# Five or six row tiles by address, shared by two queues, in a DIN recommender kernel

## The chip, the cores and the metric

The kernel runs on one core of a Trainium2 chip. The metric is the device time of one execution in microseconds (us). The median of three runs before the change is 31,618.79 us (31,618.49 to 31,619.22).

The engines are named as in the profile: PE (TensorE, with PEld for its weight loads), DVE (VectorE), ACT (ScalarE), POOL (GpSimd) and SP (SyncE). DMAs are issued by POOL, SP and ACT; ACTq and SPq are the instruction queues of ACT and SP, where an issued DMA appears.

## The reference

The inputs are 16,384 examples: an item, a category and a user id each, and a history of 200 item ids. Every id picks a row of 64 float32 values (256 bytes) from a table. For each of the 200 positions l, attention weights are computed for all 16,384 examples:

```
h   = i_emb[hist[l]]                      # 16384 x 64
x   = [h, it, h - it, h * it] @ au_W1 + au_b1      # it = i_emb[item], 36 columns
x   = dice(x)                             # normalised over the batch, sigmoid gate, alpha
w   = x @ au_W2 + au_b2
cur = cur + w * h
```

`dice(x)` normalises x over the whole batch, takes the sigmoid p of that, and gives p*x + (1-p)*alpha*x. After the history, a head of three layers (80, 40 and 2 columns), the first two with dice, works on user, item, category and `cur`. So the work is 200 times a gather of 16,384 rows, two small matrix products, and statistics over the batch.

## The kernel before

**Tiles.** The 16,384 examples are 128 tiles of 128. They are worked on in ND = 8 chunks of 16 tiles; a chunk is one (128 partitions x 1024) array after transposition. A step k is chunk c = k % 8 of position l = k // 8; the whole history is 1,600 steps. A loop (`For_i`, L455 and `steps`) runs four times over LPB = 45 positions, the last 20 positions and the head follow it.

**Where the rows come from.** `fetch(k)` gathers the 16 tiles of a chunk into `rows[k % 5]`, one indirect DMA on POOL per tile (L125). In four of the eight chunks (SIDES = 1, 3, 5, 7) the last tile is not gathered: `has_side`. Its 128 rows come one by one, 256 bytes each, by plain DMAs whose address is loaded from SBUF into a register (`addresses`, L268). The row numbers of these tiles are loaded per l (`load_addresses`), and multiplied by the row length on DVE (`scale_addresses`, L146) two steps later. Tiles of chunks 1 and 5 are SP's (`rows_by_sync`, L280, 32 rows per step, LOAD = 16 addresses per load, asked three steps ahead by `ask`), into `side`. Tiles of chunks 3 and 7 are ACT's (`rows_by_scalar`, L291, 32 rows per step in two halves, GROUP = 8 addresses per load), into `aside`. A semaphore per buffer of `aside` counts ACT's rows; `await_rows_by_scalar` waits for all 128. `turn(k)` then copies the tile into its place in `rows` on ACT (L339).

**A step.** The order on each engine is the order of the program (`manual_schedule`). Step k issues, in this order: fetch(k); gate(k-10) on ACT (sigmoid, L312) and weights(k-10), which is a product on DVE (L315) and the `wb` matmuls; half of ACT's rows; hidden(k-2) on ACT (L323, from `px` to `xs`) and measure(k-2), the batch statistics on DVE (L328); the other half of ACT's rows; turn(k-1): copy, four transposes on DVE (L154) and the `ph` and `px` matmuls; weigh(k-10) on DVE (L319, L320); product(k-1), a product on DVE (L345) and its `px` matmuls. After the last chunk of an l, moments() (L351 to L170) turns the statistics into scale and shift, with a root on ACT (L168), before gate reads them. LAG = 10 buffers `hT` and XR = 9 buffers `xs` carry a chunk from hidden to weigh.

**The head.** After the history, 256 gathers of category and user rows, then the three layers. In the second, `dice` for the first layer's second part (two arrays, `ab`) comes first; then per chunk a dice (L522 to L524), two matmuls with `w2a` over 128 rows (L538) and two with `w2b` over the 32 rows that belong to the chunk (L539), alternating; ACT moves the result out (L541) and DVE takes its statistics (L467).

Of the kernel before, what the change touches and what calls it, by code (L numbers as in the profile page):

```python
# [9 lines left out]
I32 = mybir.dt.int32  # L10
# [4 lines left out]
P = 128  # L15
D = 64
# [3 lines left out]
CD = 2 * CH  # L20
LPB = 45
ROWS = 5
LAG = 10
XR = 9
IDX = 3
BY_SP = (1, 5)
BY_ACT = (3, 7)
SIDES = (1, 3, 5, 7)
LOAD = 16
GROUP = 8  # L30
ROW = 4 * D
U8 = mybir.dt.uint8

# [2 lines left out]
def din_kernel(  # L36
# [32 lines left out]
    ZA = P // 2  # L69
    ZB = Z1 - ZA  # L70
    NS = len(SIDES)
    NB, NA = len(BY_SP), len(BY_ACT)
    serial = iter(range(10**6))
    NC = NT - NS
    BODY = L - L % LPB if L > LPB else 0
# [37 lines left out]
    idx = [make(f"idx{i}", P, NC, dt=I32) for i in range(IDX)]  # L113
    ids = [make(f"ids{i}", P, NT, dt=I32) for i in range(3)]
    side = [make(f"side{i}", P, D) for i in range(3)]
    aside = [make(f"aside{i}", P, D) for i in range(3)]
    landed = [tc.alloc_semaphore(f"landed{i}") for i in range(3)]
    addrs = make("addrs", 2 * S + 1, NS * P, dt=I32)
    addr = [addrs[i * S : i * S + 1] for i in range(3)]
    stats = [make(f"st{i}", P, 2 * ND, STATS) for i in range(3)]  # L120
    rstds = [make(f"rs{i}", P, 1) for i in range(3)]
# [15 lines left out]
    def load_hist_ids(i, l):  # L137
        nc.sync.dma_start(
            idx[i], r_hist[ds(l, 1), : NC * P].rearrange("l (p n) -> p (l n)", n=NC)
        )  # L140

    def load_addresses(i, l):
        nc.sync.dma_start(addr[i], r_hist[ds(l, 1), NC * P :])
# [74 lines left out]
    w1a = make("w1a", P, 4, P)  # L218
    w1b = make("w1b", P, 4, S)
    w2a = make("w2a", P, P)  # L220
    w2b = make("w2b", P, P)
    w3 = make("w3", P, 4, P)
    b1a = make("b1a", P, 1)
    b1b = make("b1b", S, 1)
# [9 lines left out]
    def head_weights():  # L234
        for t in (w1a, w1b, w2a, w2b, w3, bias2, al2):
            nc.vector.memset(t, 0.0)
        w1 = W1.rearrange("(f d) z -> d f z", d=D)
        for e in range(2):
            for g in range(2):
                r, d = quarter(e, g), ts(e, S)  # L240
                nc.sync.dma_start(w1a[r, :, ts(g, ZA)], w1[d, :, :ZA])
                nc.sync.dma_start(w1b[r, :, ts(g, ZB)], w1[d, :, ZA:])
        for g in range(2):
            nc.sync.dma_start(w2a[ts(g, ZA), g * ZA : g * ZA + Z2], W2[:ZA])
            nc.sync.dma_start(b1a[ts(g, ZA)], col(b1)[:ZA])
            nc.sync.dma_start(ala[ts(g, ZA)], col(alpha1)[:ZA])
            nc.sync.dma_start(b1b[ts(g, ZB)], col(b1)[ZA:])
            nc.sync.dma_start(bias2[g * ZA : g * ZA + Z2], col(b2))
            nc.sync.dma_start(al2[g * ZA : g * ZA + Z2], col(alpha2))
            for j in range(4):  # L250
                r = slice(j * S + g * ZB, j * S + (g + 1) * ZB)
                nc.sync.dma_start(w2b[r, g * ZA : g * ZA + Z2], W2[ZA:])
                w = j * S + g * ZO
                nc.sync.dma_start(w3[g * ZA : g * ZA + Z2, j, w : w + ZO], W3)
                nc.sync.dma_start(alb[r], col(alpha1)[ZA:])
        nc.sync.dma_start(bias3, b3.partition_broadcast(P))
        for t, u in ((ala, al1a), (alb, al1b), (al2, al12)):
            nc.vector.tensor_scalar(u, t, -1.0, 1.0, ALU.mult, ALU.add)

        for t, n in ((same_a, ZA), (same_b, ZB)):  # L260
            nc.vector.tensor_single_scalar(lane, lanes, n - 1, ALU.bitwise_and)
            nc.vector.tensor_copy(t, lane)
            nc.vector.tensor_scalar(t, t, 0.0, n / P, ALU.is_equal, ALU.mult)

    flat = i_emb.rearrange("v d -> (v d)").bitcast(U8)

    def addresses(l, s, p0, n, engine):
        _, at = nc.values_load_multi_w_load_instructions(  # L268
            addr[l % 3][:, s * P + p0 : s * P + p0 + n],
            engines=(engine,), min_val=0, max_val=ROW * (V - 1),  # L270
            skip_runtime_bounds_check_because="the DMA checks the address against the table",
        )
        return [flat[ds(a, ROW)].rearrange("(o d) -> o d", o=1) for a in at]

    def rows_by_sync(m, part, n):
        l, j = divmod(m, NB)
        s, dst = SIDES.index(BY_SP[j]), side[m % 3].bitcast(U8)
        for p0 in range(part * n, part * n + n, LOAD):
            for j, row in enumerate(addresses(l, s, p0, LOAD, mybir.EngineType.SP)):
                nc.sync.dma_start(dst[p0 + j : p0 + j + 1], row)  # L280


    keys = {}

    def rows_by_scalar(m, part):
        l, j = divmod(m, NA)
        s, dst = SIDES.index(BY_ACT[j]), aside[m % 3].bitcast(U8)
        key = keys.setdefault(m, f"rows{next(serial)}")
        for j, row in enumerate(addresses(l, s, part * GROUP, GROUP, mybir.EngineType.Activation)):
            p = part * GROUP + j  # L290
            dma = nc.scalar.dma_start(dst[p : p + 1], row).then_inc(landed[m % 3], 16)  # L291
            tc.no_tile_sem_insts.add(dma.ins.name)
            tc.add_to_no_dep_group(key, dma.ins)

    def await_rows_by_scalar(m):
        if m in keys:
            fence = nc.scalar.wait_ge(landed[m % 3], 16 * P)
            tc.declare_fence(fence.ins, group=keys.pop(m))
            nc.scalar.sem_clear(landed[m % 3])

    def has_side(k):
        return k % ND in SIDES

    def fetch(k):
        l, c = divmod(k, ND)
        for n in range(TD - has_side(k)):
            j = column(c, n)
            gather(rows[k % ROWS], idx[l % IDX][:, j : j + 1], n, i_emb)

    def gate(k):  # L310
        i = k // ND % 3
# [15 lines left out]
        for i in range(2):  # L327
            nc.vector.bn_stats(stats[l % 3][:, 2 * c + i, :], xs[k % XR][:, ts(i, CH)])  # L328

    def turn(k):  # L330
        if has_side(k):
            l, c = divmod(k, ND)
            if c in BY_ACT:
                m = l * NA + BY_ACT.index(c)
                await_rows_by_scalar(m)
                of = aside[m % 3]
            else:
                of = side[(l * NB + BY_SP.index(c)) % 3]
            nc.scalar.copy(rows[k % ROWS][:, TD - 1], of)  # L339
        transpose(hT[k % LAG], rows[k % ROWS])  # L340
        layer(ph, [(unit, hT[k % LAG])])
        layer(px, [(blk_h, hT[k % LAG]), (blk_i, itT[k % ND])], last=False)
# [25 lines left out]
    def step(k, last=None):  # L368

        def has(j):  # L370
            return last is None or j <= last

        if has(k):
            fetch(k)
        if has(k - LAG):
            gate(k - LAG)
            weights(k - LAG)
        if has(k):
            scalar_rows(k, 0)
        if has(k - 2):  # L380
            hidden(k - 2)
            measure(k - 2)
        if has(k):
            scalar_rows(k, 1)
        if has(k - 1):
            turn(k - 1)
        if has(k - LAG):
            weigh(k - LAG)
        if has(k - 1):
            product(k - 1)  # L390
        if has(k - 2) and (k - 2) % ND == ND - 1:
            moments((k - 2) // ND)

    AHEAD = ND // NB - 1 - BY_SP[0]

    def ask(k, end):
        m, part = divmod(k + 1 + AHEAD, ND // NB)
        if m < end * NB:  # L400
            rows_by_sync(m, part, P * NB // ND)

    def scalar_rows(k, slot):
        m, part = divmod(k, ND // NA)
        n = P * NA // ND // GROUP
        for i in range(n)[slot::2]:
            rows_by_scalar(m, part * n + i)

    def steps(l0, n, end):
        for k in range(n * ND):  # L410
            l, c = divmod(k, ND)
            if c == 0 and l + 1 < end:
                load_hist_ids((l + 1) % IDX, l0 + l + 1)
            if c == 2 and l + 1 < end:
                load_addresses((l + 1) % 3, l0 + l + 1)
            if c == 4 and l + 1 < end:
                scale_addresses((l + 1) % 3)
            ask(k, end)
            step(k)

    with tc.manual_schedule():
# [4 lines left out]
        load_ids(ids[2], r_user)  # L426
        nc.gpsimd.iota(lanes, pattern=[[1, P]], base=P, channel_multiplier=-1)
        attention_weights()
        for t in (*hT, *xs, *side, *aside, hm):
            nc.vector.memset(t, 0.0)  # L430
        for t in curT:
            nc.vector.memset(t, 0.0)
# [14 lines left out]
            if c:  # L447
                transpose(itT[c - 1], rows[(c - 1) % ROWS])
        nc.vector.memset(rows[-1 % ROWS], 0.0)
        for k in range(-1 - AHEAD, 0):  # L450
            ask(k, L)
        head_weights()

    if BODY:
        with tc.For_i(0, BODY, LPB) as l0:  # L455
            with tc.manual_schedule():
                steps(l0, LPB, LPB + 1)
                await_rows_by_scalar(LPB * NA - 1)

    K = (L - BODY) * ND  # L460
    za = [hT[(K - LAG + c) % LAG] for c in range(ND)]
# [28 lines left out]
    with tc.manual_schedule():  # L490
# [36 lines left out]
        z2 = itT  # L527
        na, nb = head_moments(0, same_a), head_moments(1, same_b)
        ab = ucT[:2]
        for j in range(2):  # L530
            dice(ab[j], zb[j], nb, al1b, alb)
        for c in range(ND + 1):
            if c < ND:
                dice(curT[c], za[c], na, al1a, ala)
                q = ts(c % 4, S)
                for h in range(2):
                    cols = ts(h, CH)
                    nc.tensor.matmul(pz[c % 4][:, cols], w2a, curT[c][:, cols], start=True, stop=False)  # L538
                    nc.tensor.matmul(pz[c % 4][:, cols], w2b[q], ab[c // 4][q, cols], start=False, stop=True)  # L539
            if c:  # L540
                nc.scalar.activation(z2[c - 1], pz[(c - 1) % 4], AF.Identity, bias=bias2)  # L541
                measure_head(2, c - 1, z2[c - 1])

        n2 = head_moments(2, same_a)
        for c in range(ND):
# [56 lines left out]
```

## Time and profile before

| | |
|---|---|
| median of the runs | 31,618.79 us |
| the profiled execution's own time | 31,616.96 us |
| its span, first to last instruction | 31,615.1 us |
| mean granted clock of PE | 0.81 |
| gathers on POOL, history | 24,800 of 944 ns |
| gathers on POOL, items and head | 384 (3 x 128) |
| row DMAs on ACT, on SP | 51,200 and 51,200 |
| DMA share of 16 engines, gathers | 11.8% |

The busy time of an engine leaves out register loads and the issue of DMAs: for ACT and SP, whose queues issue 102,400 row DMAs, it has to be read from the queue rows of the timeline. For POOL the time from the start of one gather to the start of the next matters, not the busy time alone. The page cuts the span into 40 slices; they are alike from second to last, so a stretch from the middle stands for the history.

### The profile page before, as it was taken

To read this page: it belongs to the slowest core of one execution; us is meant where nothing else is said; L and a number is where in the kernel's file an instruction comes from. 1 tells how busy PE (TensorE), PEld (TensorE's weight loads), DVE (VectorE), ACT (ScalarE), POOL (GpSimd) and SP (SyncE) were. 2 spreads that over 40 slices of the span, in tenths; PEclk is the share of its full clock that TensorE was granted. 3 is DMA by queue.
4 is the path that set the end of the run, shared out by engine and by line. 5 is a ranking of instruction groups with operands and counts; after the bars stand their busy time and mean duration, and the time that the engine had idled before them with its cause. 6 is when DMAs were issued, how large, how long until landed. Compare 5 with 4: busy or idle time off the path is not lost. (4 is left out here: it accounts for less than half of the span.)

```text
span 31615.1 us, 357535 instructions
## 1 busy us (share of the span) xinstructions
PE 20448.2 (65%) x38864; PEld 8357.2 (26%) x38864; DVE 15015.4 (47%) x18963; ACT 4479.6 (14%) x4670; POOL 23766.1 (75%) x25189
## 2 busy tenths in 40 slices
PE   5666666666666666666666666666666666666666
PEld 2222222222222222222222222222222222222222
DVE  4444444444444444444444444444444444444443
ACT  1111111111111111111111111111111111111111
POOL 7777777777777777777777777777777777777776
PEclk7888888888888888888888888888888888888887
DMA  1111111111111111111111111111111111111111
GB/s 29 28 28 28 28 28 28 28 28 28 28 28 28 28 28 28 28 28 28 28 28 28 28 28 28 28 28 28 28 28 28 28 28 28 28 28 28 28 28 23
DMA packets 1050292, 890.26 MB, mean 28 GB/s; under 512 B 644640, under 2 KB 644640, under 8 KB 1047784
## 3 DMA queue, kind: packets, MB, share of 16 engines
q0 software_dynamic: 805888, 826.84, 11.8%
q1 hardware_dynamic: 138920, 27.05, 0.4%
q10 hardware_dynamic: 102976, 13.32, 0.3%
q14 instruction: 2202, 18.04, 0.2%
q8 instruction: 306, 5.01, 0.1%
HBM read 865.03 MB, written 0.13 MB: 27 GB/s over the span
## 5 line engine op out<-in xcount | busy, mean ns | idle before, releaser
L125 POOL DMA_INDIRECT rows<-in_L_rec_i_emb,idx x24800 | 23403.2, 944 | 7593.5 <-issue 7032.1
L159 PE MATMUL ph<-hT,unit 128*128 128x512 f32 x6404 | 5658.4, 1029 | 10498.9 <-DVE hT L154 10498.9
L154 DVE STREAM_TRANSPOSE hT<-rows 64x512 f32<-64x512 f32 x6404 | 4518.8, 706 | 8256.8 <-DMA rows<-in_L_rec_i_emb,idx 4150.3
L328 DVE BATCH_NORM_STATS2 st<-xs 128x6 f32<-128x512 f32 x3204 | 2060.4, 685 | 7172.9 <-ACT xs L323 7172.9
L159 PEld LDWEIGHTS ph<-hT,unit 128*128 128x128 f32 x6404 | 1688.5, 295 | 13506.4 <-DVE hT L154 13334.4
L159 PE MATMUL px<-hT,blk_h 128*128 128x512 f32 x6404 | 3936.6, 702 | 0.0
L323 ACT ACTIVATE xs<-px,au_bias 128x1024 f32<-128x1024 f32 x1602 | 1784.3, 1114 | 14626.1 <-PE px L159 12323.9
L159 PE MATMUL wb<-y,blk_p 128*128 128x512 f32 x6440 | 3329.8, 599 | 455.3 <-DVE y L315 455.3
L159 PE MATMUL px<-itT,blk_i 128*128 128x512 f32 x6404 | 3368.8, 608 | 0.0
L159 PE MATMUL wb<-xs,blk_x 128*128 128x512 f32 x6440 | 3307.3, 595 | 51.5 <-PEq L455 39.9
L159 PE MATMUL px<-hm,blk_m 128*128 128x512 f32 x6408 | 3013.0, 592 | 40.5 <-DVE hm L430 40.5
L312 ACT ACTIVATE pg<-xs,sh,rs 128x1024 f32<-128x1024 f32 x1610 | 1939.8, 1205 | 3751.2 <-issue 2579.9
L315 DVE TENSOR_TENSOR y<-pg,xs 128x1024 f32<-128x1024 f32 x1610 | 1956.6, 1215 | 512.9 <-ACT pg L312 508.6
L159 PEld LDWEIGHTS px<-hT,blk_h 128*128 128x128 f32 x6404 | 1566.7, 245 | 2295.1 <-issue 2294.6
L319 DVE SCALAR_TENSOR_TENSOR wb<-wb,au_bias,hT 128x1024 f32<-128x1024 f32 x1610 | 2080.5, 1292 | 88.2 <-PE wb L159 36.0
L320 DVE TENSOR_TENSOR curT<-wb,curT 128x1024 f32<-128x1024 f32 x1610 | 1970.8, 1224 | 54.8
L345 DVE TENSOR_TENSOR hm<-ph,itT 128x1024 f32<-128x1024 f32 x1601 | 1941.2, 1212 | 0.0
L159 PEld LDWEIGHTS px<-itT,blk_i 128*128 128x128 f32 x6404 | 1374.9, 215 | 1925.3 <-issue 1925.3
L159 PEld LDWEIGHTS wb<-y,blk_p 128*128 128x128 f32 x6440 | 1212.0, 191 | 2081.7 <-issue 1445.9
L159 PEld LDWEIGHTS wb<-xs,blk_x 128*128 128x128 f32 x6440 | 1228.3, 191 | 1603.9 <-issue 1597.9
L159 PEld LDWEIGHTS px<-hm,blk_m 128*128 128x128 f32 x6408 | 1218.1, 190 | 1573.0 <-issue 1424.7
L339 ACT COPY rows<-aside 128x64 f32<-128x64 f32 x401 | 97.9, 244 | 2659.6 <-DMA aside<-in_L_rec_i_emb 2525.7
(155 smaller groups left out, 2171.5 us busy)
## 6 DMA issues: line engine op xcount, KB each, us to landing
aside<-in_L_rec_i_emb ACTq DMA_DIRECT2D x51200, 0.2 KB
side<-in_L_rec_i_emb SPq DMA_DIRECT2D x51200, 0.2 KB
rows<-in_L_rec_i_emb,idx POOLq DMA_INDIRECT x24800, 2.4
idx<-in_r_hist SPq DMA_DIRECT2D x200, 62.0 KB
addrs<-in_r_hist SPq DMA_DIRECT2D x200, 2.0 KB
rows<-in_L_rec_i_emb,ids POOLq DMA_INDIRECT x128, 2.4
rows<-in_L_rec_c_emb,ids POOLq DMA_INDIRECT x128, 2.4
rows<-in_L_rec_u_emb,ids POOLq DMA_INDIRECT x128, 2.4
```

Source lines behind the costliest of these rows:

```text
L125: nc.gpsimd.indirect_dma_start(out=dst[:, n, :], out_offset=None, in_=table, in_offset=bass.IndirectOffsetOnAxis(ap=ids, axis=0),)
L154: nc.vector.transpose(by_tile(dst[ts(e, D)], i), of[ts(i, D), :, ts(e, S)])
L159: nc.tensor.matmul(dst[:, ts(i, CH)], lhsT, rhs[:, ts(i, CH)], start=(first and j == 0), stop=(last and j == len(pairs) - 1), skip_group_c ...
L312: nc.scalar.activation(pg, xs[k % XR], AF.Sigmoid, bias=shifts[i], scale=rstds[i])
L315: nc.vector.tensor_mul(y, pg, xs[k % XR])
L319: nc.vector.scalar_tensor_tensor(wb, wb, au_bias2, hT[k % LAG], ALU.add, ALU.mult)
L320: nc.vector.tensor_add(curT[k % ND], wb, curT[k % ND])
L323: nc.scalar.activation(xs[k % XR], px, AF.Identity, bias=au_bias)
L328: nc.vector.bn_stats(stats[l % 3][:, 2 * c + i, :], xs[k % XR][:, ts(i, CH)])
L339: nc.scalar.copy(rows[k % ROWS][:, TD - 1], of)
L345: nc.vector.tensor_mul(hm, ph, itT[k % ND])
```

## The change

The change moves more tiles from POOL to the two row queues, puts both queues on the same tile, and rearranges the step and the second layer of the head.

- SIDES becomes (1, 3, 4, 5, 6, 7), with SOMETIMES = 5 and EACH = 3: chunk 5's last tile comes by address only where l % 3 == 0. So six tiles come by address in every third l, five in the others. In these, chunk 5's last tile is gathered with ids of its own (`sidx`, loaded by `load_side_ids`).
- `rows_by_address(k)` takes the place of `rows_by_sync`, `rows_by_scalar`, `ask` and `scalar_rows`. Each step asks for a step's share (an eighth) of the l's own rows, half on SP and half on ACT: 40 each with five tiles, 48 with six. Addresses are loaded 20 at a time (16 with six tiles). Both write to the three buffers `side`; the semaphore counts the rows of both.
- `place(k)`, the wait and the copy, is taken out of turn and stands in front of the step's rows on ACT. hidden(k-2) goes to the front of the step, gate follows it, weights goes to the end beside weigh, after product. measure(k-2) follows turn(k-1), but in the step that ends an l it comes first, with moments().
- LAG becomes 9 and XR 8, `aside` is dropped.
- In the second layer `w2b` is laid out as four 128-row matrices that are zero outside a chunk's 32 rows, so all matmuls have 128 rows. The dice of `ab` comes when it is first needed, and the move out of PSUM is two chunks behind.

```diff
-LAG = 10
-XR = 9
+LAG = 9
+XR = 8
 IDX = 3
-BY_SP = (1, 5)
-BY_ACT = (3, 7)
-SIDES = (1, 3, 5, 7)
-LOAD = 16
-GROUP = 8
+SIDES = (1, 3, 4, 5, 6, 7)
+SOMETIMES = 5
+EACH = 3
+LOAD = 20
...
+    def load_side_ids(i, l):
+        j = column(SOMETIMES, TD - 1)
+        nc.sync.dma_start(sidx[i], r_hist[ds(l, 1), j * P : (j + 1) * P].rearrange("l p -> p l"))
...
+    def rows_by_address(k):
+        l, s = divmod(k, ND)
+        first, tiles = tiles_by_address(l)
+        n = len(tiles) * P // ND // 2
+        loads = -(-n // LOAD)
+        for i, (engine, issue) in enumerate(
+            ((mybir.EngineType.SP, nc.sync), (mybir.EngineType.Activation, nc.scalar))
+        ):
+            r0, end = (2 * s + i) * n, (2 * s + i + 1) * n
+            while r0 < end:
+                many = min(end - r0, -(-n // loads))
+                at0 = tiles[r0 // P] * P + r0 % P
+                while tiles[(r0 + many - 1) // P] * P + (r0 + many - 1) % P != at0 + many - 1:
+                    many -= 1
+                _, at = nc.values_load_multi_w_load_instructions(
+                    addr[l % 3][:, at0 : at0 + many],
...
+                for r, a in enumerate(at, r0):
+                    m, p = first + r // P, r % P
+                    key = keys.setdefault(m, f"rows{next(serial)}")
+                    dma = issue.dma_start(
+                        side[m % 3].bitcast(U8)[p : p + 1],
+                        flat[ds(a, ROW)].rearrange("(o d) -> o d", o=1),
+                    ).then_inc(landed[m % 3], 16)
...
     def has_side(k):
-        return k % ND in SIDES
+        l, c = divmod(k, ND)
+        return c in SIDES and (c != SOMETIMES or l % EACH == 0)
...
+        ends = (k - 2) % ND == ND - 1
         if has(k):
             fetch(k)
+        if has(k - 2):
+            hidden(k - 2)
+            if ends:
+                measure(k - 2)
+                moments((k - 2) // ND)
         if has(k - LAG):
             gate(k - LAG)
-            weights(k - LAG)
+        if has(k - 1):
+            place(k - 1)
         if has(k):
-            scalar_rows(k, 0)
-        if has(k - 2):
-            hidden(k - 2)
-            measure(k - 2)
-        if has(k):
-            scalar_rows(k, 1)
+            rows_by_address(k)
         if has(k - 1):
             turn(k - 1)
-        if has(k - LAG):
-            weigh(k - LAG)
+        if has(k - 2) and not ends:
+            measure(k - 2)
         if has(k - 1):
             product(k - 1)
-        if has(k - 2) and (k - 2) % ND == ND - 1:
-            moments((k - 2) // ND)
...
+        if has(k - LAG):
+            weights(k - LAG)
+            weigh(k - LAG)
...
-        for j in range(2):
-            dice(ab[j], zb[j], nb, al1b, alb)
-        for c in range(ND + 1):
+        for c in range(ND + 2):
             if c < ND:
                 dice(curT[c], za[c], na, al1a, ala)
-                q = ts(c % 4, S)
-                for h in range(2):
-                    cols = ts(h, CH)
-                    nc.tensor.matmul(pz[c % 4][:, cols], w2a, curT[c][:, cols], start=True, stop=False)
-                    nc.tensor.matmul(pz[c % 4][:, cols], w2b[q], ab[c // 4][q, cols], start=False, stop=True)
-            if c:
-                nc.scalar.activation(z2[c - 1], pz[(c - 1) % 4], AF.Identity, bias=bias2)
-                measure_head(2, c - 1, z2[c - 1])
+                layer(pz[c % 4], [(w2a, curT[c])], last=False)
+                if c % 4 == 0:
+                    dice(ab[c // 4], zb[c // 4], nb, al1b, alb)
+                layer(pz[c % 4], [(w2b[:, c % 4], ab[c // 4])], first=False)
+            if c >= 2:
+                nc.scalar.activation(z2[c - 2], pz[(c - 2) % 4], AF.Identity, bias=bias2)
+                measure_head(2, c - 2, z2[c - 2])
```

## The prediction

> **What bounds the kernel now.** I read the page's busy shares and costliest groups first, then the waits, then the timeline in three places: ACT's own rows in mid-kernel, SP's, and the end of the kernel.
>
> ```profile
> PE 20448.2 (65%) x38864; PEld 8357.2 (26%) x38864; DVE 15015.4 (47%) x18963; ACT 4479.6 (14%) x4670; POOL 23766.1 (75%) x25189
> ...
> L125 POOL DMA_INDIRECT rows<-in_L_rec_i_emb,idx x24800 | 23403.2, 944 | 7593.5 <-issue 7032.1
> ...
> POOL rows L125 <- issue: 7142.1, 23320, 9.3
> ...
> POOL rows L125 <- DMA rows<-in_L_rec_i_emb,idx: 548.0, 1797, 0.3
> ...
> 7129.46 0.94 POOL L125 DMA_INDIRECT rows<-in_L_rec_i_emb,idx  x1 [0.30 <-issue]
> 7139.70 0.94 POOL L125 DMA_INDIRECT rows<-in_L_rec_i_emb,idx  x1 [9.30 <-issue]
> 7140.95 0.94 POOL L125 DMA_INDIRECT rows<-in_L_rec_i_emb,idx  x1 [0.30 <-issue]
> ```
>
> POOL looks 75% busy but is full. A gather takes 944 ns and the gap before the next is 0.30 us, "issue", so gathers start every 1.249 us (7139.70 to 7140.95 is one such step). The waits put down to DMAs are also 0.3 us each at most: that gap under another name. The only larger gaps are four turns of the loop: from single records 10.25, 8.46, 8.45 and 3.9 us between starts, 26 us beyond the usual. The account closes: 24,800 gathers plus 384 for items and head are 25,184 x 1.249 = 31,455; plus 2.9 before the first, 26 at the turns and 136 after the last start (31477.85) makes 31,620 against a span of 31,615.1. So time is the number of gathers, and what follows the last.
>
> ```profile
> 15018.10 1.11 ACT L323 ACTIVATE xs<-px,au_bias 128x1024 f32<-128x1024 f32 x1 [9.41 <-PE px L159]
> 15018.96 6.68 ACTq L291 DMA_DIRECT2D aside<-in_L_rec_i_emb  x16
> ...
> 15045.20 0.24 ACT L339 COPY rows<-aside 128x64 f32<-128x64 f32 x1 [6.20 <-DMA aside<-in_L_rec_i_emb]
> 15045.35 1.20 ACT L312 ACTIVATE pg<-xs,sh,rs 128x1024 f32<-128x1024 f32 x1
> 15046.09 6.65 ACTq L291 DMA_DIRECT2D aside<-in_L_rec_i_emb  x16
> ...
> SPq L268 <- DVE addrs L146: 6115.7, 132, 48.4
> SPq L268 <- DVE y L315: 3216.8, 66, 49.7
> 15153.09 25.15 SPq L280 DMA_DIRECT2D side<-in_L_rec_i_emb  x64
> ```
>
> The page's 14% for ACT leaves out its queue (ACTq). Sixteen row DMAs take 6.2 to 6.7 us there, and 0.86 us pass between an activation's start and the first row: the load of eight addresses into registers. The queue goes on while an activation runs (15045.35 lasts 1.20, the rows start 0.74 into it), so an activation costs the queue almost nothing. SP waits 9,332 us for addresses, 30% of the span, and needs 25.15 us for 64 rows with the loads between them.
>
> ```profile
> 31504.35 2.05 PE L538 MATMUL px<-curT,w2a 128*128 128x512 f32 x2 [9.48 <-issue]
> 31506.33 2.07 PE L539 MATMUL px<-ucT,w2b 32*128 32x512 f32 x2
> 31508.33 2.08 PE L538 MATMUL px<-curT,w2a 128*128 128x512 f32 x2
> 31510.33 2.07 PE L539 MATMUL px<-ucT,w2b 32*128 32x512 f32 x2
> ```
>
> In the second layer every switch between a 128-row and a 32-row matmul costs: one starts each 2.0 us.
>
> **The change, part by part.**
>
> *Gathers.* Before, 124 per l. After, 122 where six tiles come by address and 123 where five do. Four bodies of 45 l and a tail of 20 have 4 x 15 + 7 = 67 l of the first kind and 133 of the second: 8,174 + 16,359 = 24,533, which is 267 fewer. 267 x 1.249 = **-333.5 us**, on the path, as POOL is never starved.
>
> *Row DMAs on ACT.* 256 rows per l for both queues become 768 or 640 shared evenly: 48 or 40 per step on each. Prices from ACT's single records: row to row 0.3165 us (median 0.307); from a load's first row to the second 0.555, so 0.24 extra; load to first row 0.945 for 8 addresses, and 1.364 on SP for 16. That is 0.052 per address, so I estimate 1.36 for ACT's loads of 16 and 1.57 for 20. With six tiles: 384 x 0.3165 + 24 x (0.24 + 1.36) = 160; events and dispatch of two activations and a copy about 3; the wait at the moments about 6 (activation 1.11, two statistics 1.3, aggregate to variance 2.25, root 0.3, then reciprocal and shift; bounds 5.4, and 8 if the 2.5 of L319 and L320 stand before it). Together 169, against POOL's 122 x 1.249 = 152.4. With five: 320 x 0.3165 + 17 x 1.81 + 3 + 6 = 141 (the 17th load is at the skipped column), against 153.6. Three l: **ACT 451, POOL 459.6**, a margin of 9 us or 2%.
>
> ACT falls 16 us behind in each first l and wins 25 back in the next two. What takes the lag up is the ring of five rows buffers: a gather of step k waits for the transposes of k-5, which now end some 5 us after the gathers of that step, so 4 x 19.1 - 5 = 71 us stand free. I take ACT at nothing. Its bounds: with row to row at 0.307, ACT needs 441; at 0.337 (the mean while SP issues too, every long interval counted) 472.
>
> *SP.* 48 rows with three loads: 3 x (1.364 + 0.367 + 14 x 0.33 + 0.28) = 19.9 us; 40 with two 16.3. Three l with index, address and the new sidx loads (0.43 each, as for a 128x1 load of ids at the start): about 435, 95% of POOL. Behind SP stand only rows; behind a late row stand ACT's wait in place(), then DVE's transposes. Price nothing by the same ring.
>
> *Order and buffers.* LAG 10 to 9, XR 9 to 8, and weights behind product. On DVE one step is still 2.9 + 1.4 + 1.2 + 1.2 + 1.3 + 1.2 = 9.2 us. L339's activation of k-2 writes the buffer that the wb matmuls of k-10 read at the end of step k-1, so it starts after them: in the trace the last wb matmul ended 13.8 us after the transposes began (15007.62 to 15021.44). With the 2.5 of weigh that chain is 16.3 per step, under 19.1. Price nothing; covered by POOL, at 16.3 of 19.1. The SP look-ahead (ask) goes: each tile is now asked within its own l, one step or more before place(). At loop exit SP first issues the head's weights (21 us, 28061 to 28082): the ring again. The scale of 768 addresses, not 512, adds about 0.2 us of DVE per l, hidden.
>
> *Second layer.* 32 matmuls at 2.0 are 64 us (31504.35 to 31568.5). All with 128 rows and no switch they start 0.86 us apart, as the wb ones do in mid-kernel: 27.5. Then DVE is last: ten dice of 2.03 (L523 0.81, L524 1.22) and eight pairs of statistics of 1.29 are 30.6 from 31498.2; with the last matmuls, activation (1.1) and statistics behind curT[7], the end of L467 moves from 31570.97 to about 31531: **-40 us**. Bounds: 0 if the switch was not the cause, -42 if DVE alone counts.
>
> *Turns of the loop.* 26 us stay, since after two five-tile l ACT has caught up; if it has not, up to one step each, 4 x 19 = 77.
>
> Sum: 31,615.1 - 333.5 - 40 = 31,242 of span. The profiled run's own time is 1.8 above its span and the runs' median 1.8 above that (31,618.79): **31,246 us**, 1.2% faster. Its own range is 31,215 to 31,330.
>
> [...] The row first: ACT's median from row to row is 0.308 us with SP issuing within 0.4 us and 0.307 alone; SP's is 0.323 both ways. [...] Were the 0.217 us of each row exclusive, a pair would take 0.434, ACT 120 us more per three l, and the kernel some 38,000 us; the row speaks against that, and I go by it.
>
> **Rivals.**
>
> *ACT becomes the bound.* For it: 2% is a thin margin, the loads of 20 addresses are an extrapolation, and both queues now issue nearly all the time, not SP 70% of it. Against: the 0.307 above. Place: ACTq in rows_by_address, whence late place() and late transposes. At 0.337 per row ACT needs 472 per three l: 12.4 over POOL, 67 times = 830 us, and about 60 at the turns: **32,130 us**, slower. It decides from 459.6 on; from 465 on (0.330 per row) the loss eats the whole gain.
>
> *The step's chain becomes the bound.* hidden(k-2) behind wb(k-10), product behind ph: if the chain of 16.3 were 19.4, 1,600 steps x 0.3 = 480 us more: **31,730 us**. Against: its matmul spacings are measured, and 2.8 us are free.
>
> *It does not do what it says:* POOL's gathers grow with more DMAs in flight and eat the 333. At 1.262 (the 99th percentile now) 24,917 gathers cost 324 more: **31,570 us**. Against: 1.249 holds in stretches with and without rows.
>
> **How the numbers follow.** Forecast 72%; ACT as bound 19%, a sixth of it still under 31,550; the chain 5%; larger gathers 4%. The range 31,215 to 31,680 takes in the forecast, the mild part of ACT as bound and the larger gathers: some 81%. What this kernel's measurement tells from no change is 0.2%, 63 us. Faster: 72 + 3, 75%; same: half of the gathers' rival and a little of ACT's, 4%; slower: 21%.
>
> **What would show it.** Right: 24,533 gathers still 1.249 us apart, no POOL gap over 1 us but the turns, ACTq idle some 2%, about 40 us less after the last gather, wb matmuls of the second layer near 0.86 apart. Wrong: POOL's rows waiting for DVE hT (the ring is empty), with ACTq solid from six-tile l to six-tile l; or turns of 30 us and more.

## The result, and the profile after

The changed kernel takes 31,252.28 us in the median of four runs (31,247.28 to 31,267.21), the kernel before 31,618.9: a ratio of 0.9885, with a 95% interval of 0.9868 to 0.9902. It is 1.2% faster; 31,246 was forecast. The profiled execution is the slowest of the four, 31,267.21 us with a span of 31,265.4. One execution of the kernel with the old second layer, below, took 44,256 us at a granted clock of 0.528 in place of 0.80 and is left out of its median.

The first lines are the busy shares and the group of the gathers, from the page of the changed kernel; then its waits on POOL (us in total, times, longest us).

```profile
PE 20664.2 (66%) x38856; PEld 8483.2 (27%) x38856; DVE 15126.3 (48%) x18955; ACT 4402.8 (14%) x4941; POOL 23531.5 (75%) x24922
...
L123 POOL DMA_INDIRECT rows<-in_L_rec_i_emb,idx x24400 | 23043.1, 944 | 7477.2 <-issue 7226.7
```

```profile
POOL rows L123 <- issue: 7379.5, 24090, 17.2
POOL rows L123 <- DMA rows<-in_L_rec_i_emb,idx: 171.5, 562, 0.3
POOL rows L123 <- DVE hT L156: 16.8, 55, 0.3
```

POOL is as full as before. The 24,400 gathers here and 133 by `sidx` make 24,533, and the gap between two is still 0.3 us. No wait for DVE hT is longer than that: the ring of rows buffers was never empty. The larger gaps are the four turns of the loop: 17.2 us at the first, 4.4, 4.5 and 3.2 at the others. Here is the first in POOL's timeline (start, duration, and in brackets the idle time before):

```profile
7060.08 0.94 POOL L123 DMA_INDIRECT rows<-in_L_rec_i_emb,idx  x1 [0.30 <-issue]
7078.19 0.94 POOL L123 DMA_INDIRECT rows<-in_L_rec_i_emb,idx  x1 [17.16 <-issue]
7079.43 0.94 POOL L123 DMA_INDIRECT rows<-in_L_rec_i_emb,idx  x1 [0.30 <-issue]
```

The second layer in PE's timeline, where x4 in a row are two of the matmuls that had a row with x2 each before:

```profile
31195.82 1.88 PE L161 MATMUL ph<-curT,w2a 128*128 128x512 f32 x4
31197.54 1.88 PE L161 MATMUL ph<-ucT,w2b 128*128 128x512 f32 x4
31199.26 1.88 PE L161 MATMUL pg<-curT,w2a 128*128 128x512 f32 x4
```

These rows start 1.72 us apart, so one matmul takes 0.86; before, one took 2.0.

The difference of the two spans can be split up from single records. Of 349.7 us (31,615.1 to 31,265.4), 267 gathers x 1.249 are 333.5, and the time after the last gather's start fell from 137.3 (for which the prediction has 136) to 97.8, 39.5. Against that the turns cost 28.1 in place of 26.1, gathers longer than 1 us cost 20.0 in place of 2.7, and the 3.9 that remain are the spread of all other starts: 333.5 + 39.5 - 2.0 - 17.3 - 3.9 = 349.8.

ACT in mid-kernel, in its timeline (ACTq rows are runs of row DMAs; the time in brackets counts as idle also what the queue spends on issuing):

```profile
15089.70 1.11 ACT L339 ACTIVATE xs<-px,au_bias 128x1024 f32<-128x1024 f32 x1 [16.18 <-DVE wb L335]
15090.83 1.28 ACT L170 ACT_TABLE_LOAD   x1
15094.63 0.29 ACT L170 ACTIVATE std<-var,eps 128x1 f32<-128x1 f32 x1 [2.52 <-DVE var L380]
15094.94 1.28 ACT L328 ACT_TABLE_LOAD   x1
15096.24 1.21 ACT L328 ACTIVATE pg<-xs,sh,rs 128x1024 f32<-128x1024 f32 x1
15096.90 14.98 ACTq L301 DMA_DIRECT2D side<-in_L_rec_i_emb  x40
15111.98 1.11 ACT L339 ACTIVATE xs<-px,au_bias 128x1024 f32<-128x1024 f32 x1 [14.53 <-issue]
```

This is a step that ends an l. From 15089.70 to 15096.90 the queue issues no rows, because of the moments; then it issues 40 rows and their loads, and the next step's hidden starts 0.1 us behind them. In all steps, the time in which ACT had issued its rows and waited for px is 201 us, 0.6% of the span. POOL sets the time, and ACT is close behind it.

### The profile page after: what moved, and what is told of

Same layout as the page of the kernel before. It is cut to its first block, busy times and chain, and to the rows that moved or that the text cites. A ratio compares the mean times of both kernels' runs of the same rounds, so it can differ in the third digit from the quotient of the medians.

```text
span 31265.4 us, 423966 instructions
## 1 busy us (share of the span) xinstructions
PE 20664.2 (66%) x38856; PEld 8483.2 (27%) x38856; DVE 15126.3 (48%) x18955; ACT 4402.8 (14%) x4941; POOL 23531.5 (75%) x24922
## 3 DMA queue, kind: packets, MB, share of 16 engines
q0 software_dynamic: 797344, 818.07, 14.9%
## 5 line engine op out<-in xcount | busy, mean ns | idle before, releaser
L123 POOL DMA_INDIRECT rows<-in_L_rec_i_emb,idx x24400 | 23043.1, 944 | 7477.2 <-issue 7226.7
L161 PE MATMUL ph<-hT,unit 128*128 128x512 f32 x6404 | 5876.4, 1065 | 10398.4 <-DVE hT L156 10395.6
L161 PE MATMUL px<-hT,blk_h 128*128 128x512 f32 x6404 | 4090.6, 727 | 0.0
L161 PEld LDWEIGHTS px<-hT,blk_h 128*128 128x128 f32 x6404 | 1641.9, 256 | 2404.6 <-issue 2394.2
L352 ACT COPY rows<-side 128x64 f32<-128x64 f32 x1068 | 249.0, 233 | 327.0 <-DMA side<-in_L_rec_i_emb 197.0
```

Source lines behind the costliest of these rows:

```text
L123: nc.gpsimd.indirect_dma_start(out=dst[:, n, :], out_offset=None, in_=table, in_offset=bass.IndirectOffsetOnAxis(ap=ids, axis=0),)
L161: nc.tensor.matmul(dst[:, ts(i, CH)], lhsT, rhs[:, ts(i, CH)], start=(first and j == 0), stop=(last and j == len(pairs) - 1), skip_group_c ...
```

## Experiments

All times are medians, beside runs of the kernel before on the same chip (31,618 to 31,621 us). The kernels ran on several chips, so a difference of some 3 us between two of them tells nothing.

**Five tiles in every l.** This changes the number of gathers and takes the load off ACT.

```diff
+SIX = ()
...
-        return c in SIDES and (c != SOMETIMES or l % EACH == 0)
+        return c in SIDES and (c != SOMETIMES or l % EACH in SIX)
```

> Five tiles by address in every l, never six: 123 gathers per l, 24,984 with items and head, 67 more than the changed kernel; ACT has 141 us of work per l against POOL's 153.6. If POOL's gathers alone set the time: 67 x 1.249 = 84 us slower than the changed kernel, 31,336 us. If the six-tile l already cost ACT more than the ring of rows buffers hides, taking them out gives something back: less than 31,300 us, and the trace of the changed kernel's gaps on POOL shrinks by more than its turns.

Measured 31,334.87 us, 82.6 more than the changed kernel (ratio to before 0.991, 0.9894 to 0.9925). The law of the gathers holds to 1 us; ACT now waited 2,302 us for px and this bought nothing.

**Six tiles in two of three l.**

```diff
+SIX = (0, 1)
-LOAD = 20
+LOAD = 24
...
-        return c in SIDES and (c != SOMETIMES or l % EACH == 0)
+        return c in SIDES and (c != SOMETIMES or l % EACH in SIX)
```

> Six tiles in two of every three l (67 gathers fewer than the changed kernel), addresses loaded 24 at a time, which makes ACT's six-tile l cheaper (two loads per step for three). If POOL alone set the time it would be 31,252 - 84 = 31,168 us. By the prediction's ACT account three l now cost ACT 2 x 163 + 141 = 467 us against POOL's 458.4: 8.6 us too much, 67 times, 31,740 us (31,500 to 31,950), with POOL's rows waiting for DVE hT.

Measured 32,625.83 us (ratio 1.0316, 1.0302 to 1.0331): slower than before, although it has 67 gathers fewer than the changed kernel. The rival "ACT becomes the bound" lies one notch away. Its waits:

```profile
POOL rows L124 <- issue: 7370.1, 23510, 64.2
...
POOL rows L124 <- DVE hT L157: 1390.3, 521, 6.9
...
ACT rows L353 <- DMA side<-in_L_rec_i_emb: 284.1, 148, 7.5
```

POOL waits for the transposes (DVE hT), up to 6.9 us each, and at every turn 64 us: ACT's lag fills the whole ring. But the size was off by 886 us. A mean step takes 20.05 us here without the turns, 481 per three l, of which ACT waits for px only about 1; the account said 467. Its timeline at the start of an l shows a part that was left out:

```profile
15112.75 1.20 ACT L329 ACTIVATE pg<-xs,sh,rs 128x1024 f32<-128x1024 f32 x1
15118.36 0.24 ACT L353 COPY rows<-side 128x64 f32<-128x64 f32 x1 [4.41 <-DMA side<-in_L_rec_i_emb]
15120.18 18.42 ACTq L302 DMA_DIRECT2D side<-in_L_rec_i_emb  x48
```

The copy of place() stands 4.41 us for the rows of the l's last tile, which both queues finished asking for only at the end of the step before. All of the next 48 rows are queued behind it.

**The same, with the rows asked a step ahead.**

```diff
-        if has(k):
-            rows_by_address(k)
+        for j in asked:
+            rows_by_address(j)
...
-            step(k)
+            step(k, asked=[j for j in ((0, 1) if k == 0 else (k + 1,)) if j < n * ND])
```

> The kernel with six tiles in two of three l, with each step asking for the rows of the next step's share (the first step of a stretch asks for two). In that kernel place() at the start of an l stood 3 to 4 us on ACT for the last tile's rows, which both queues had only just issued; asked a step ahead they have landed. If this wait is the part of ACT's account that was left out, ACT's three l fall from 484 to about 474 us: 67 x 10 = 660 us less, about 31,960 us, with no wait of ACT for rows. If that wait only stands where another would, it stays at 32,600.

Measured 32,074.01 us (ratio 1.0143, 1.0126 to 1.016), 552 less, or 8.3 us per three l where 10 were expected. The wait of the copy for rows is gone from its list of waits. So this wait is more than half of the 14 us by which the account was short. Without it ACT's 24 steps still take 472 us, 5 over the account. From each load's first row to the next load, or to hidden, there are 363 us per three l where the account had 356, and from the loads to their first rows 86 where it had 84; events and moments take 22 in place of 27.

**24 addresses per load.**

```diff
-LOAD = 20
+LOAD = 24
```

> The changed kernel with 24 addresses per load: in the six-tile l two loads per step in place of three, 0.8 us per step less on ACT and on SP, 6 us per six-tile l; the five-tile l are as they were. If POOL sets the time: unchanged, 31,252 us within 15, with more idle time on ACT (400 us in all). If ACT sets it anywhere but at the turns, faster by up to 400 us.

Measured 31,253.0 us (ratio 0.9884, 0.9869 to 0.9899): no change. ACT's wait for px grew from 201 to 358 us. In its profiled execution the first turn took 6.0 us, not 18.1; which of the two a run gets, and whether ACT's small reserve decides it, was not tested by itself.

**The second layer of before, and its 128-row layout alone.** In the first, `w2b` and the loop are those of the kernel before. In the second only the layout is kept from the change; the lines are shown against the kernel before:

```diff
-                    nc.tensor.matmul(pz[c % 4][:, cols], w2b[q], ab[c // 4][q, cols], start=False, stop=True)
+                    nc.tensor.matmul(pz[c % 4][:, cols], w2b[:, c % 4], ab[c // 4][:, cols], start=False, stop=True)
```

> The changed kernel with the second layer of the kernel before (32-row matmuls between 128-row ones, the dice of ab ahead of the loop, the move out one chunk behind). By the account of the tail 40 us slower, 31,292 us, with 137 us after the last gather's start in place of 98, and its matmuls 2.0 us apart. If the tail shrank for another reason, such as the rows ending earlier, it stays at 31,252.

> The changed kernel with the second layer's order of before (both dice of ab ahead of the loop, matmuls alternating, the move out one chunk behind), but with w2b laid out over 128 rows. If the switch between row counts was the cause of the 2.0 us spacing: its 32 matmuls start 0.86 us apart and nearly the whole gain of the tail is there, 100 to 106 us after the last gather's start and 31,255 to 31,262 us. If the order was the cause: near 137 us, and 31,292.

Measured 31,292.87 us (ratio 0.9896, 0.9881 to 0.9911) and 31,262.27 us (0.9887, 0.9871 to 0.9904). The first is 41 us slower than the changed kernel, with 137.0 us after the last gather's start; the second 10 us, with 107.2. The second layer in the timeline of the first, then of the second:

```profile
31204.97 2.08 PE L540 MATMUL ph<-curT,w2a 128*128 128x512 f32 x2
31206.97 2.07 PE L541 MATMUL ph<-ucT,w2b 32*128 32x512 f32 x2
31208.98 2.08 PE L540 MATMUL ph<-curT,w2a 128*128 128x512 f32 x2
```

```profile
31200.27 1.02 PE L539 MATMUL ph<-curT,w2a 128*128 128x512 f32 x2
31201.13 1.02 PE L540 MATMUL ph<-ucT,w2b 128*128 128x512 f32 x2
...
31205.03 1.10 PE L539 MATMUL pg<-curT,w2a 128*128 128x512 f32 x2 [1.16 <-ACT itT L542]
```

With the same order, 2.0 us become 0.86 when the 32-row form goes, which takes 29.8 us off the tail (137.0 to 107.2). Most of this is PE's granted clock, the 0.50 and 1.00 in these rows (stretch, its length, PE's busy time and records, clock, DMA share, GB/s), in the first and then in the second:

```profile
31197.00:31260.00 63.00, 63.00 (x63) 0.50 0.00 0
```

```profile
31194.00:31199.00 5.00, 4.95 (x6) 0.50 0.00 0
31201.00:31227.00 26.00, 22.53 (x52) 1.00 0.00 1
```

The second layer of the kernel before is at 0.50 too, from end to end (31503.90 to 31568.50); that of the changed kernel is at 1.00 from 31193.8 on, 3 us after its first matmul. With 128 rows alone the first matmuls, at 0.50, start 1.70 us apart:

```profile
31195.89 1.92 PE L540 MATMUL px<-ucT,w2b 128*128 128x512 f32 x2
31197.59 1.91 PE L539 MATMUL px<-curT,w2a 128*128 128x512 f32 x2
```

So at the same clock the switch costs 0.3 us of the 2.0; the step from 1.70 to 0.86 is the clock, which rises to 1.00 only where the 32-row form is gone. What in that form keeps it down is not shown. The other 9.4 (107.2 to 97.8) come from the order: in the last row PE stands 1.16 us for ACT's move out of PSUM, one chunk behind, which the changed kernel has two chunks behind.

**The step's order of before.** The order, LAG and XR as they were:

```diff
-LAG = 9
-XR = 8
+LAG = 10
+XR = 9
...
+        if has(k - LAG):
+            gate(k - LAG)
+            weights(k - LAG)
         if has(k - 2):
             hidden(k - 2)
-            if ends:
-                measure(k - 2)
-                moments((k - 2) // ND)
-        if has(k - LAG):
-            gate(k - LAG)
+            measure(k - 2)
         if has(k - 1):
             place(k - 1)
...
-        if has(k - 2) and not ends:
-            measure(k - 2)
+        if has(k - LAG):
+            weigh(k - LAG)
         if has(k - 1):
             product(k - 1)
-        if has(k - LAG):
-            weights(k - LAG)
-            weigh(k - LAG)
+        if ends and has(k - 2):
+            moments((k - 2) // ND)
```

> The changed kernel with the order within a step of before (gate and weights first, weigh behind turn, moments last; LAG 10, XR 9), rows and second layer as changed. The prediction priced the new order at nothing: 31,252 us within 20, with ACT's waits within a step still hidden. If the new order is needed to keep ACT free (the trace of the changed kernel shows ACT waiting for px only 201 us in all, 0.13 us per step, so little is left), a wait of one microsecond more per step would add 1,600 - 200 = 1,400 us: 32,600.

Measured 31,251.66 us (ratio 0.9884, 0.9867 to 0.99): no difference. The whole rearrangement of the step is worth nothing here.

**The scaling on DVE.** In single records of the changed kernel 94 gathers last longer than 1 us, 20.0 us more than 944 ns each in all; 93 of them overlap `scale_addresses`, which has 768 elements for 512 before (32 long gathers, 2.7 us). One of them, POOL's timeline and then DVE's:

```profile
3637.58 0.94 POOL L123 DMA_INDIRECT rows<-in_L_rec_i_emb,idx  x1 [0.30 <-issue]
3638.83 1.29 POOL L123 DMA_INDIRECT rows<-in_L_rec_i_emb,idx  x1 [0.30 <-issue]
3640.43 0.94 POOL L123 DMA_INDIRECT rows<-in_L_rec_i_emb,idx  x1 [0.31 <-issue]
```

```profile
3638.75 0.55 DVE L148 TENSOR_SCALAR addrs<-addrs 1x768 int32<-1x768 int32 x1
```

Three kernels tested it: nine operations for one, a two-input operation in its place, and no such operation on DVE at all.

```diff
+        for _ in range(8):
+            nc.vector.tensor_scalar_mul(dummy, addr[i], 1)
```

> The changed kernel with the scaling of the addresses on DVE followed by eight copies of the same operation into a tile that nobody reads (576 to 580 ns each, 4.6 us of DVE per l). In the changed kernel 93 of its 94 gathers longer than 1 us overlap this operation, by 213 ns on average. If the operation holds up POOL's gathers: 8 x 200 operations x 0.47 x 0.21 us = 160 us slower or more, 31,400 us, with some 800 long gathers; if it held them for its whole time, up to 930 us. If the overlap is by chance, or DVE only delays others, 31,252 us and about 94 long gathers.

```diff
-        nc.vector.tensor_scalar_mul(addr[i], addr[i], ROW)
+        nc.vector.scalar_tensor_tensor(addr[i], addr[i], float(ROW), addr[i], ALU.mult, ALU.max)
```

> The changed kernel with the addresses scaled by a two-input operation on DVE, max(256 a, a), in place of the multiplication by a constant; once per l as before. Eight more of the constant multiplications did not make more gathers long, so either the first operation of a burst alone matters or the operation is a bystander. If the constant multiplication is the cause: the 80 to 94 gathers over 1 us go, 16 to 20 us less, 31,235 us. If it is a bystander, or a two-input operation holds POOL as well: as many long gathers as before and 31,252 us.

The third scales on ACT, loads 24 addresses at a time and asks a step ahead:

```diff
-        nc.vector.tensor_scalar_mul(addr[i], addr[i], ROW)
+        nc.scalar.mul(addr[i], addr[i], float(ROW))
```

> The changed kernel's six tiles in every third l (24,917 gathers), with the addresses scaled on ACT (about 1 us per l) in place of DVE, 24 addresses per load, and rows asked a step ahead, which make room for it on ACT: 3 l cost it about 457 + 3 - 10 = 450 us against POOL's 459.6. If DVE's operation is what holds POOL's gathers, hardly any gather over 1 us is left and the kernel takes 31,252 - 16 = 31,236 us. If it is a bystander, 80 to 94 long gathers and 31,252. The runs with six tiles in 7 of 15 and 2 of 3 l had row packets of 54 to 125 ns in place of 16 and POOL waiting for DMAs: if that comes with more rows per us (4.37 here, 4.46 and 4.57 there), the queues of the row DMAs keep near 0.7% here; if it comes with asking ahead, their share doubles at least and the time is 31,300 or more.

Measured: nine times 31,641.29 us (1.0007, 0.9997 to 1.0017), two inputs 31,283.05 (0.9893, 0.9878 to 0.9908), on ACT 31,235.06 (0.9879, 0.9862 to 0.9895).

The last two settle the cause. Without the operation on DVE one long gather is left, the very first, and the time is 17 us under the changed kernel's, the 16 expected; its four runs (31,233.55 to 31,237.78) lie wholly below those of the changed kernel. With a 946 ns operation in place of 580, 132 gathers are long by 53.4 us in all, and the kernel is 31 us slower. This version on ACT is the fastest of the study. (24 addresses per load alone changed nothing; asking ahead alone in this version was not run.)

The run with nine missed on both counts: 85 long gathers, no more than with one, and yet 389 us more. DVE's timeline in it shows why no more gathers were held:

```profile
3057.46 0.55 DVE L149 TENSOR_SCALAR addrs<-addrs 1x768 int32<-1x768 int32 x1
3058.05 4.90 DVE L151 TENSOR_SCALAR dummy<-addrs 1x768 int32<-1x768 int32 x8
```

Eight in 4.90 us are one each 0.61, half of POOL's 1.249. In the changed kernel an operation held a gather when it started 0.3 to 0.6 us (36 of 59) or 0.9 to 1.25 us (55 of 60) after a gather's start, and almost never elsewhere (1 in 79). Of the 1,584 extra operations in the loop 1,344 started 0.1 to 0.2 or 0.6 to 0.7 us after one: once in step with POOL, they fall between. The 389 us are another matter: each turn lasted 58 to 63 us, 242 in all in place of 28, and POOL's other waits in this run make 170. Their way is argued, not tested: 4.9 us of DVE per l delay the wb matmuls, hidden waits for these, and ACT's lag fills the ring.

**Two more fractions, in the old order and asked ahead.** The first is 2 of 3; the second, with the two-input scaling too, has

```diff
-EACH = 3
-LOAD = 20
+EACH = 15
+SIX = (0, 2, 4, 6, 8, 10, 12)
+LOAD = 24
```

> Six tiles in two of three l, 24 addresses per load, rows asked a step ahead, and the order within a step of before. In the run asked ahead ACT needed 475 us per three l; of them 5.4 us per l are hidden, statistics, moments and root one behind the other, which in the old order lie behind the rows of a step; there the root and two table loads leave 2.9. So ACT falls by 2.5 x 3 = 7.5 to 468 us against POOL's 458.4: 31,168 + 67 x 9.4 = 31,800 us. If the waits of the old order (gate behind rows, hidden behind gate) come on top, 32,070 or more; if it hides more than I count, POOL at 31,168.

> A version meant to beat both: six tiles in 7 of 15 l (94 of 200, 27 gathers fewer than the changed kernel), 24 addresses per load, rows asked a step ahead, the step order of before, and the two-input scaling. ACT: 7 x 163 + 8 x 139 = 2,253 us per fifteen l against POOL's 2,296, 2% free. So POOL sets the time: 31,252 - 27 x 1.249 = 31,218 us; 31,202 if the long gathers go as well. If ACT's waits in the old order are dearer than counted, above 31,300.

Measured 31,760.51 us (1.0044, 1.0031 to 1.0058) and 31,370.38 us (0.9921, 0.9908 to 0.9935). The first number came out as expected, but not for the reason given, and the second missed by 150 to 170 us. POOL's timeline in the second:

```profile
777.00 0.95 POOL L124 DMA_INDIRECT rows<-in_L_rec_i_emb,idx  x1 [0.30 <-issue]
...
781.22 0.94 POOL L124 DMA_INDIRECT rows<-in_L_rec_i_emb,idx  x1 [0.66 <-DMA rows<-in_L_rec_i_emb,idx]
783.01 0.94 POOL L124 DMA_INDIRECT rows<-in_L_rec_i_emb,idx  x1 [0.85 <-DMA rows<-in_L_rec_i_emb,idx]
```

Here POOL waits mostly for DMAs, not for transposes: with 7 of 15, 254 gathers start 1.3 to 3.3 us after the one before, which costs 103 us, and with 2 of 3 some 1,520, which costs 587 us; the profile puts 215 and 1,246 of these down to DMAs. With the long gathers of the two-input scaling (49) and the turns (31) the first account closes: 24,890 x 1.249 + 2.9 + 99.5 + 103 + 49 + 31 = 31,373, span 31,368.6. The page's DMA queues (packets, MB, share of 16 engines; q0 is POOL's, q1 SP's, q10 ACT's) of the changed kernel, of 7 of 15, and of 2 of 3:

```profile
q0 software_dynamic: 797344, 818.07, 14.9%
q1 hardware_dynamic: 193112, 31.56, 0.6%
q10 hardware_dynamic: 137440, 17.76, 0.4%
```

```profile
q1 hardware_dynamic: 192680, 32.00, 1.6%
q10 hardware_dynamic: 140896, 18.21, 1.3%
```

```profile
q1 hardware_dynamic: 192040, 32.64, 3.3%
q10 hardware_dynamic: 146016, 18.88, 3.0%
```

For 1 to 6% more bytes the packets' time rises about threefold, and five- to eightfold; a 256-byte packet takes 16.5 ns in the changed kernel, 54 and 123 ns in these two. So whether ACT's account for the old order was right remains untested: another limit came first.

## Why the prediction was right, point by point

*POOL full, the gathers counted.* Right: 1.249 us, 24,533 in the history, and the number of gathers carried to five tiles in every l (82.6 measured, 84 worked out).

*The row queues.* Right that ACT stays under POOL, too wide in the margin. The load estimates held: from a load of 20 addresses to its first row the median was 1.56 us in the kernel with five tiles always (1.57 estimated), and 1.42 for 16 in the changed kernel (1.36); row to row had a median of 0.311, with SP's 0.32 at the same time. ("256 rows per l for both queues" is what each queue had before; together they had 512.) But of "ACT 451, POOL 459.6" only 3 us per three l were free (201 us over 67 rounds), not 9: ACT needed 457. The step that was off is "each tile is now asked within its own l, one step or more before place()", with no price: the last eighth of an l's rows is asked in the step just before its place(), and ACT's queue then stands behind that copy. In the changed kernel:

```profile
15070.46 1.20 ACT L328 ACTIVATE pg<-xs,sh,rs 128x1024 f32<-128x1024 f32 x1
15073.27 0.24 ACT L352 COPY rows<-side 128x64 f32<-128x64 f32 x1 [1.61 <-DMA side<-in_L_rec_i_emb]
15074.85 14.72 ACTq L301 DMA_DIRECT2D side<-in_L_rec_i_emb  x40
```

In these steps the queue's next load starts 3.4 us after hidden (median), in the steps without such a wait, moments aside, 0.2 or less: some 10 us per three l. The rows, to the next load or to hidden, took 4 more than priced (342 for 338). Luck made up for most of it: events and moments, priced at 27 per three l, took 19 beside that wait. SP's 95% was about right: it waits some 2,160 us for buffers of `side` (1,551.9 for ACT's clearing of the semaphore and 604.9 for its copy), 7% of the span.

*The ring.* Said to hold 71 us. When ACT was too slow the turns stretched to 58 to 65 us, about what was said to lie in it.

*Order and buffers at nothing.* Right: 31,251.66 with the old order. So the rival of the step's chain is out for this kernel.

*Second layer, -40.* Right in sum (39.5 in the tail, 41 in time), but the reason was mostly another. "Every switch between a 128-row and a 32-row matmul costs" puts all of 2.0 against 0.86 down to the switch, without the clock of that stretch. At the same granted clock, 0.50, the switch is 0.3 us; the rest is the clock's rise to 1.00, which the prediction took over from mid-kernel without saying so (1.00 from 15013 to 15021 us of the kernel before), and which came by luck. The new layout is three quarters of the gain; the later move out is 9.4 us, which the step had put into the same price.

*Turns.* 26 were to stay; 28.1 in the profiled execution, 16 to 17 in four of the other kernels with the same gathers, 31 to 32 in two.

*The scaling.* "Adds about 0.2 us of DVE per l, hidden" was wrong in kind: the operation lengthens gathers on POOL, 17 us more than before. Nothing on DVE's side of the timeline hid it, since what it cost was POOL's. These 17 us are more than the 6 by which the median passes the forecast; where an execution's turns cost 16 in place of 26, that makes up for most of the rest.

*Larger gathers as a rival.* Out for the changed kernel: apart from the long gathers and the turns no gather starts more than 1.31 us after the one before, although the gathers' own packets take 14.9% of the 16 engines in place of 11.8%. It is real in the old order asked ahead, where POOL waited for DMAs at 4.46 and 4.57 rows per us (the changed kernel has 4.37: 136,576 in 31,265 us). That the rate is the cause is not shown.

## What to carry to other kernels

When work moves from a full engine to queues, account for the queue's waits too: look for the last item of each round, asked just before it is needed, because everything behind it in the queue waits with it (with six tiles in two of three l, 48 rows behind a copy that stood 4.41 us). A margin of under 1% on the second engine, here 3 of 459.6 us per three l, was a cliff edge: one more tile in every third l turned 1.2% faster into 3.2% slower. And an operation on an engine that is not the bound can still lengthen those of the engine that is (here by 213 ns each, 20 us in all); look at the longest members of the bound's largest group, and at what overlaps them. Where matmuls are far apart, read the granted clock of that stretch before the form of the matmul gets all the blame: here 0.3 us of 2.0 was the form at the same clock, and 0.84 the clock.

## What was not expected of the hardware

- A one-partition scaling of 768 int32 on DVE (580 ns) lengthens POOL's gathers by 213 ns on average in 93 of 200 cases, one of 946 ns with two inputs by 405 ns in 131 of 200; on ACT, none. The 580 ns operation did next to nothing at other offsets from a gather's start (1 in 79), and eight more in step with POOL made no more gathers long (85); the 946 ns one held gathers at most other offsets too (72 of 103). What holds the gathers up is not shown.
- Row packets of 256 bytes took 16.5 ns in the changed kernel, at 4.37 rows per us, and many times that in the old order asked ahead: 54 ns at 4.46 (7 of 15), 123 at 4.57 (2 of 3). What they wait for is open. The rate is not all of it: 2 of 3 without asking ahead had 23 ns at 4.44 rows per us, 2 of 3 asked ahead in the new order 39 ns at 4.52 (there 58 us of POOL's gaps are put down to DMAs), and asking ahead with the changed kernel's rows 25 ns at 4.37 and no waits on POOL.
- PE's granted clock stayed at 0.50 through 63 us without a gap in which 128-row and 32-row matmuls alternate. With 128 rows throughout it went to 1.00 after some 5 us in the 128-row layout alone, and after 3 us in the changed kernel.
